# The first attention of a two-layer decoder: new weights for mixing the next group's maxima with the present group's units

## Chip, cores and metric

The kernel runs on one core of one Trainium2 chip. The metric is the time of one execution on the device in microseconds (us); a smaller number is better. Engines are called as in the profile: PE is TensorE, PEld its weight load, DVE is VectorE, ACT is ScalarE, POOL is GpSimd, and SP is SyncE, which here issues the transfers.

## The reference

The input x has 4 batches of 1024 tokens with 256 channels, and six blocks are applied in turn, each as `x = x + f(layernorm(x))`. Cut to what the change touches, the first of them is:

```python
def L0_attn(x, w_attn, w_proj):            # 16 heads of 16 channels, causal, with alibi
    q, k, v = split(x @ w_attn.T)          # each B x 16 x 1024 x 16
    att = q @ k.T / 4 + slopes * (pos_k - pos_q)
    att = softmax(where(pos_k <= pos_q, att, -inf))
    return (att @ v) @ w_proj.T

x = x + L0_attn(ln(x));  x = x + L0_xattn(ln(x), ctx);  x = x + L0_ffn(ln(x))   # 8-bit activations
x = x + L1_attn(ln(x));  x = x + L1_xattn(ln(x), ctx);  x = x + L1_ffn(ln(x))   # 4-bit blocks
```

The second attention (L1_attn) has squared scores with a decay for each token in place of the exponential; L0_xattn and L1_xattn attend to 77 context rows.

## The kernel before

**The first attention.** `A0(b, after)` handles batch b in four groups of four heads. For a group, `stacks` loads two stacked operands, QS (queries) and KS (keys), from DRAM; each has two buffers. The softmax's row maxima are computed ahead of the main loop: `a0_max` is a generator of 38 steps. A step is one or a few matmuls (L352, and L356 for the mask) into a PSUM tile M of one bank, and a reduction by DVE (L357) into the tile mt. M has two banks, 2 and 3, in turn, shared with the tiles Q of the projections. After 11 steps, and again at the end, `a0_put_max` negates the maxima, transposes them (L381), splits them in two bf16 parts (L383, L384) and sends them by two transfers each into rows 108 and 109 of QS, so that the score matmuls of the main loop subtract them.

`a0_main` is the main loop of a group: 20 units. A unit computes scores of four heads for one block of keys and up to 256 queries into two PSUM tiles S (L401, mask L403; banks 0 and 1 in turn), ACT takes the exponential (L404) into P, and two units later PE multiplies P by the values (L413) into O. `o_out` normalizes.

The weaving is done by generators. While group g runs its 20 units, `nxt(g + 1)` loads the stacks of the next group and yields its 38 maxima steps. In group 2, 12 steps of `after` are mixed in as well, and in group 3 the rest of `after` runs. For batches 0 to 2 `after` is `A0_front(b + 1)`, the projections of the next batch (18 steps) and the maxima of its group 0 (38 steps); for batch 3 it is the front of the second attention. The function that mixes takes the next step from the generator that is least far along relative to its weight:

```python
def weave(a, na, b, nb):
    live = {0: (a, na), 1: (b, nb)}
    ...
        k = min(live, key=lambda k: done[k] / live[k][1])
        try:
            next(live[k][0])
...
            yield from weave(self.a0_main(st, V, y, g, O, pend), 20, side, self.NW[b][g])
```

The main loop's weight is 20, the number of its units; the side's weight is `NW[b][g]`. When one generator ends, the other goes on alone.

**Around it.** `schedule` runs the four `A0` in turn, each woven with the cross attention `XA` (L616 to L637) and feed-forward `F0` (L697 to L754; its down projection is L747, L749, L752) of the batch before, at fixed weights. After that, in the second phase, come the second attention `A1` (scores L898, absolute values by DVE L904 or ACT L902, square L906, decay L909 on POOL, value matmuls L927) woven with `XA` and the last feed-forward `F1`. `A1` uses two banks for its scores as well. Splits in high and low parts are recorded under a helper's lines, L179 and L180, and the three-matmul products under L191.

**Order.** The order in which Python emits instructions isn't the order in which the engines run them: the program is built in `tile.TileContext(nc, schedule_with_timeline_sim=True)`, which places the instructions of each engine's queue itself, within the dependencies, and takes the emission order as a preference. Each engine then runs its queue in order.

Of the kernel before, what the change touches and what calls it, by code (L numbers as in the profile page):

```python
# [90 lines left out]
class Kern:  # L91
    MAGIC = 12582912.0
    LAG0, LAG1 = 2, 2
    GQ, NQ = (2, 2, 2, 2), (12, 12, 12, 12)
    NW = ((25, 25, 38, 38),) * 4

    def const(self, *names):
        for nm, dt in names:
# [371 lines left out]
    def A0(self, b, after):  # L470
# [10 lines left out]
        for g in range(4):  # L481
            box = []
            side = nxt(g + 1, box) if g < 3 else after
            if g == self.GQ[b]:
                side = weave(side, 28, take(after, self.NQ[b]), self.NQ[b])
            yield from weave(self.a0_main(st, V, y, g, O, pend), 20, side, self.NW[b][g])
            if g < 3:
# [670 lines left out]
def take(g, n):  # L1158
    for _ in range(n):
        if next(g, g) is g:  # L1160
            return
        yield


def weave(a, na, b, nb):

    live = {0: (a, na), 1: (b, nb)}
    done = [0, 0]
    while live:
# [3 lines that stand above are left out]
            done[k] += 1  # L1173
        except StopIteration:
            del live[k]
        yield
# [149 lines left out]
```

## Time and profile before

| | us |
|---|---|
| median of 3 runs | 2410.97 (2407.53 to 2416.93) |
| the profiled execution's own time | 2408.58 |
| its span, first to last instruction | 2406.8 |
| PE busy | 2141.5 (89%) |
| DVE busy | 1692.2 (70%) |
| ACT busy | 1639.2 (68%) |
| POOL busy | 1198.2 (50%) |

In the trace the four main loops of batch 0 lie between 105 and 335 us, batches 1 to 3 each take a little over 300 us until 1274 us, the second attention runs until 2260 us, and the feed-forward of the last batch ends the span. A row of waits names the engine and tile that waited, the engine and tile that ended the wait, the sum in us, the number of waits and the longest one. A row of a timeline has start, duration and engine, and in brackets the idle time ahead of it with what ended it.

### The profile page before, as it was taken

What the parts mean: (1) busy time and instruction counts of PE and PEld (TensorE: products, weight loads), DVE (VectorE), ACT (ScalarE), POOL (GpSimd) and SP (SyncE); (2) the same over time, 40 slices, a digit from 0 to 9 for tenths busy, and PEclk for the clock granted to TensorE, in tenths of its full rate; (3) what the DMA queues carried; (4) which work ended last, traced back from release to release, by engine and by line L of the source; (5) the groups of instructions that cost most, each with busy time, mean ns of one, the idle gap of its engine ahead of it and who ended that gap; (6) DMA issues with size and microseconds to landing.
All of it is one profiled execution on the core that took longest, in us unless ns stands there. A gap on an engine that the chain in (4) does not pass through costs nothing.

```text
span 2406.8 us, 51445 instructions
## 1 busy us (share of the span) xinstructions
PE 2141.5 (89%) x19110; PEld 1510.9 (63%) x19110; DVE 1692.2 (70%) x3781; ACT 1639.2 (68%) x4173; POOL 1198.2 (50%) x1942
## 2 busy tenths in 40 slices
PE   6798899998999998899988988889988998899876
PEld 4454457755666654576656766567766766676675
DVE  4666657677766786776775677777867787777766
ACT  4365446676766676565778878987678777888542
POOL 7121313154331352412545458766867788775664
PEclk9899999999999999899989999999989999999988
DMA  8667331223841236231262224512241223542000
GB/s 260 199 193 211 116 90 44 66 61 108 242 135 44 64 111 188 69 73 41 81 185 53 71 71 129 149 38 56 98 111 43 56 74 119 105 98 71 10 10 18
DMA packets 182697, 238.45 MB, mean 99 GB/s; under 512 B 16198, under 2 KB 165846, under 8 KB 175958
## 3 DMA queue, kind: packets, MB, share of 16 engines
q1 hardware_dynamic: 182446, 235.15, 34.8%
q8 instruction: 151, 2.47, 0.4%
q14 instruction: 100, 0.82, 0.1%
HBM read 152.62 MB, written 82.21 MB: 98 GB/s over the span
## 4 chain that ended last, share of the span: by engine, by line
PE 59%; DVE 14%; DMA 8%; POOL 7%; ACT 7%; issue 3%; SPq 1%; POOLq 0%; DVEq 0%; ACTq 0%
PE T L191 10%; PE W L191 8%; PE O L413 7%; PE O L927 5%; PE S L401 5%; PE Q L191 4%; PE M L352 4%; PE S L898 3%; DVE P L904 2%; DVE s_mt L357 2%; PE W L630 1%; PE T L723 1%; DMA wst<-in_L_xattn_Wq 1%; POOL P L909 1%; ACT P L906 1%
## 5 line engine op out<-in xcount | busy, mean ns | idle before, releaser
L357 DVE TENSOR_REDUCE s_mt<-M 128x1 f32<-128x512 f32 (+3 forms) x608 | 386.2, 655 | 137.9 <-PE M L356 100.0
L404 ACT ACTIVATE P<-S 128x512 f32<-128x512 f32 (+1 forms) x640 | 342.4, 563 | 154.7 <-PE S L401 78.5
L906 ACT ACTIVATE P<-P,eps 128x1024 f32<-128x1024 f32 x320 | 344.5, 1082 | 57.2 <-DVE P L904 52.6
L904 DVE TENSOR_REDUCE P<-S 128x512 f32<-128x512 f32 (+1 forms) x480 | 284.8, 610 | 75.4 <-PE S L898 60.7
L352 PE MATMUL M<-KS,QS 108*128 108x512 bf16 (+3 forms) x768 | 225.8, 341 | 48.2 <-DVE s_mt L357 23.9
L191 PE MATMUL T<-R,xX 128*128 128x352 f32 (+1 forms) x1136 | 246.7, 331 | 4.8 <-ACT E L619 1.4
L898 PE MATMUL S<-QS,KS 96*128 96x256 bf16 (+1 forms) x1280 | 217.9, 269 | 36.9 <-DVE P L904 34.5
L401 PE MATMUL S<-QS,KS 110*128 110x256 bf16 (+1 forms) x1280 | 230.4, 267 | 16.9 <-ACT P L404 13.7
L413 PE MATMUL O<-P,V 128*32 128x256 f32 (+1 forms) x2560 | 240.1, 377 | 0.8 <-ACT P L404 0.6
L622 POOL TENSOR_TENSOR E<-E,s_xsm 128x616 f32<-128x616 f32 x64 | 77.9, 1217 | 323.7 <-DVE s_xsm L620 261.3
L191 PEld LDWEIGHTS T<-R,xX 128*128 128x128 f32 x1136 | 183.0, 190 | 24.7 <-ACT E L619 5.4
L191 PE MATMUL W<-R,xph 128*128 128x256 f32 (+1 forms) x952 | 185.4, 292 | 6.5 <-DVE xpl L180 4.8
L909 POOL TENSOR_TENSOR P<-P,y 128x512 f32<-128x512 f32 x128 | 165.1, 1299 | 34.0 <-ACT y L871 17.4
L619 ACT ACTIVATE E<-T,s_xmx 128x77 f32<-128x77 f32 x512 | 159.6, 334 | 28.6 <-DVE s_xmx L616 26.5
L401 PEld LDWEIGHTS <-KS 110*128 110x128 bf16 x1280 | 107.2, 100 | 105.6 <-issue 60.3
L927 PE MATMUL O<-P,VsJ 128*32 128x128 f32 x3584 | 168.2, 282 | 5.3 <-ACT P L906 4.8
L898 PEld LDWEIGHTS <-KS 96*128 96x128 bf16 x1280 | 101.8, 99 | 110.2 <-issue 88.9
L191 PEld LDWEIGHTS W<-R,xph 128*128 128x128 f32 (+1 forms) x952 | 149.5, 192 | 17.8 <-DVE xpl L180 6.9
L352 PEld LDWEIGHTS <-QS 108*128 108x128 bf16 x768 | 68.3, 100 | 128.0 <-issue 100.4
L191 PE MATMUL W<-R,xpl 128*128 128x256 f32 (+2 forms) x476 | 139.6, 293 | 1.0 <-DVE xpl L180 1.0
L730 POOL TENSOR_TENSOR R<-wst 128x256 f32<-128x256 f32 x128 | 92.3, 732 | 88.0 <-DVE wst L729 82.8
L179 ACT ACTIVATE xph<-W 128x512 fp32r<-128x512 f32 (+2 forms) x180 | 79.3, 458 | 80.1 <-PE W L633 32.8
(351 smaller groups left out, 5660.0 us busy)
## 6 DMA issues: line engine op xcount, KB each, us to landing
QS<-dr SPq DMA_DIRECT2D x144, 192.0 KB
KS<-dr SPq DMA_DIRECT2D x72, 384.0 KB
dr<-qp SPq DMA_DIRECT2D x32, 768.0 KB
MD<-R SPq DMA_DIRECT2D x24, 616.0 KB
UD<-R SPq DMA_DIRECT2D x24, 512.0 KB
R<-MD SPq DMA_DIRECT2D x32, 308.0 KB
X<-in_x SPq DMA_DIRECT2D x16, 512.0 KB
dr<-qp SPq DMA_DIRECT2D x32, 256.0 KB
```

The source lines that it names most:

```text
L191: nc.tensor.matmul(out, x, y, start=first and n == 0, stop=last and n == len(seq) - 1)
L352: nc.tensor.matmul(Sv[:, x, 0:w], QS[:108, i // 4, hh, i % 4 * 128 : i % 4 * 128 + 128], KS[:108, hh, k0:k1], start=x == 0, stop=not diag ...
L357: nc.vector.tensor_reduce(out, Sv[:, :, 0:w], AX.X, ALU.max)
L401: nc.tensor.matmul(S[:, e, 0:w], st[1][:110, hh, j * 128 : (j + 1) * 128], st[0][:110, q0 // 512, hh, q0 % 512 : q0 % 512 + w], start=e == ...
L404: nc.scalar.activation(P[:, 2 * p : 2 * p + 2, 256 - w :], S[:, :, 0:w], AF.Exp)
L413: nc.tensor.matmul(O[0][hh * 32 : hh * 32 + 32, o + o0 : o + 256], V[j // 4][:, j % 4, h * 17 : h * 17 + 32], P[:, hh, o0:], start=c % 2 = ...
L619: nc.scalar.activation(E[:, n * 77 : (n + 1) * 77], Sv[:, k, :], AF.Exp, bias=mx[:, n : n + 1], accum_out=sm[:, n : n + 1])
L898: nc.tensor.matmul(S[:, e, 0:w], st[r][1][:96, hh, j * 128 : (j + 1) * 128], st[r][0][:96, q0 // 512, hh, q0 % 512 : q0 % 512 + w], start= ...
L904: nc.vector.tensor_reduce(Pv, S[:, :, 0:w].unsqueeze(3), AX.X, ALU.max, apply_absolute_value=True)
L906: nc.scalar.activation(Pw, Pw, AF.Square, bias=self.eps1)
L909: nc.gpsimd.tensor_tensor(Pd, Pd, Ds[r, c][:, j - 2 * c], ALU.mult)
L927: nc.tensor.matmul(Oc[rows, o0 : o0 + 128], lhs, P[:, hh, c0 : c0 + 128], start=j == 2 * c and i == 2 * c, stop=fin and i == 2 * c + 1)
```

## The change

One line of constants changes: the weights of the side generators in `A0`, for all four batches. In groups 0 and 1 the weight goes from 25 to 42, in group 2 from 38 to 54 and in group 3 from 38 to 48. The counts of steps are 38 in groups 0 and 1, 38 + 12 in group 2, and 44 in group 3 (8 in batch 3), so that with the new weights every side generator is emitted to its end beside the 20 units of the main loop. What is computed, and with which instructions, stays as it is.

```diff
     GQ, NQ = (2, 2, 2, 2), (12, 12, 12, 12)
-    NW = ((25, 25, 38, 38),) * 4
+    NW = ((42, 42, 54, 48),) * 4
```

## Prediction

> **What bounds the kernel now.** The table of engines by stretch came first, cut where the attention batches change. Columns: length, then busy time of PE, PEld, DVE, ACT, POOL, then the granted clock.
>
> ```profile
> 335.00:642.00 307.00, 288.68 (x2362) 192.58 (x2361) 218.59 (x494) 207.00 (x610) 103.25 (x150) 0.99 0.33 92
> 642.00:949.00 307.00, 294.09 (x2341) 192.38 (x2341) 220.78 (x504) 204.88 (x608) 98.70 (x146) 0.98 0.40 111
> 949.00:1274.00 325.00, 296.04 (x2298) 194.18 (x2298) 230.15 (x525) 206.33 (x615) 119.84 (x182) 0.93 0.34 96
> 1274.00:1500.00 226.00, 202.85 (x2089) 149.47 (x2081) 156.57 (x388) 190.88 (x518) 135.57 (x253) 0.98 0.29 80
> ```
>
> PE is busy 94, 96 and 91% of the time in the first three rows, which are batches 1 to 3 of the first attention. It idles 18 + 13 + 29 = 60 us in 939. DVE and ACT are near 70%. After 1274 us, in the second attention, PE idles more (23 of 226 us). So I asked next what ends PE's waits.
>
> ```profile
> PE S L898 <- DVE P L904: 34.5, 58, 4.3
> PE M L352 <- DVE s_mt L357: 23.9, 49, 2.0
> PE S L401 <- ACT P L404: 13.7, 16, 3.6
> PE M L352 <- DMA KS<-c_alk: 5.4, 2, 4.4
> PE S L401 <- DMA QS<-VsJ: 2.4, 5, 0.8
> ```
>
> Columns: sum, times, longest. The second row is what the change is about: a maxima step waits until DVE has reduced the bank it is to overwrite. It costs 23.9 us in the whole kernel, in 49 of 608 steps. The first row, in the second attention, is larger. Last the timeline, at a place where maxima steps really stand alone (start, duration, engine):
>
> ```profile
> 293.58 8.20 DVE L357 TENSOR_REDUCE s_mt<-M 128x1 f32<-128x512 f32 x13
> 294.31 0.38 PE L352 MATMUL M<-KS,QS 108*128 108x512 bf16 x1 [0.22 <-DVE s_mt L357]
> 294.91 0.38 PE L352 MATMUL M<-KS,QS 108*128 108x512 bf16 x1 [0.22 <-DVE s_mt L357]
> 295.51 0.38 PE L352 MATMUL M<-KS,QS 108*128 108x512 bf16 x1 [0.22 <-DVE s_mt L357]
> ```
>
> Alone, a step comes every 0.60 us, PE works 0.38 and waits 0.22, while DVE runs its reductions (0.63 us each) without a gap.
>
> **Part one, the emission order.** A maxima generator yields 38 steps against 20 units of the main loop. At the old weights (25) about 25 of them are emitted beside the units; numbering the tiles in order of creation gives 14, 14, 12 and 7 maxima steps behind the last unit of groups 0 to 3, 181 over the 15 group boundaries. With 42, 42, 54, 48 the count is 0 everywhere. If all 181 stood alone, they would cost PE 181 x 0.22 = 40 us. The wait row says 23.9, and that is all that can be won at this place.
>
> **Part two, what the queues make of it.** The framework puts the instructions in its own order. I laid the built queues of the two kernels side by side. Behind the last score matmul of each group, PE's queue of before holds 9, 12, 21, 16 / 20, 7, 34, 16 / 19, 9, 21, 18 / 21, 5, 17 maxima steps, 245 in all. In the changed kernel it holds 9, 12, 21, 16 / 20, 3, 30, 17 / 20, 5, 19, 19 / 18, 4, 17, which is 230. So 181 moved steps become 15 in the queue. In batch 0 the main loop and the maxima stand exactly as before; the burst of the timeline is still there, twelve steps in a row. Those leftover steps mostly aren't alone: PE meets the next group's scores between them, which is why only 49 of 608 wait. Instructions, shapes and counts are the same on every engine, DMAs too: none added, none removed, so busy time is priced at nothing gained or lost. SP's queue shifts by 8 places at most. The transfer that carries a group's maxima back (QS) keeps its cover: between the last maximum and the first score that needs it, PE's queue loses 1.1 us at worst and gains up to 7, so the row of 2.4 us stays.
>
> **Part three, the price of the shuffle.** The reordering runs on to the end of the program, also where no source line moved. I priced the matmuls of each line by its busy time, overlaps counted once, over its columns (scores 0.255 us, maxima 0.288 us, scores of the second attention 0.289 us per 512 columns). Then I summed, along PE's queue, by how much the work between two uses of one thing falls short of the time that thing needs, choosing the need so that the sum of before meets its wait row.
>
> Maxima banks, need 0.9 us (a reduction of 0.65 and its signals): 24.1 before (row: 23.9), 25.9 after: +1.8.
>
> Score banks of the second attention, need 0.9 (reduction of 0.61): 32.7 before (rows: 34.5, and 1.4 behind ACT), 44.5 after: +11.8. Gaps under 0.3 us go from 25 to 41 of 640.
>
> Score banks of the first attention, need 0.9: 8.8 to 9.3, +0.5 (row: 13.7).
>
> The down projection of the first feed-forward, whose matmuls need the 1.02 us copy of L749, need 1.8: 5.6 before (row: 6.2), 11.1 after: +5.5.
>
> P before the value matmuls L927, need 2.5: 11.5 before (rows: 5.1 and 4.8), 15.5 after: +4.
>
> The KS transfer that opens a group's maxima, and can only start when the scores two groups back have let the buffer go. The two waits of the row KS <- c_alk are 1.0 and 4.4 us, at places where PE's queue holds 12.0 and 7.4 us of work between, so the need is about 12.4. In the changed queue the distances of batches 1, 2 and 3 are 9.7, 8.5 and 8.8 us (before 12.0, 13.5 and 7.4): 2.7 + 3.9 + 3.6 = 10.2 against 5.4: +4.8.
>
> The others that I summed go both ways by 1 to 2 us.
>
> The full sum is +28.4 us. It is an upper end, because a stall on PE lets DVE and ACT run ahead and so shortens the next one, and the P and down-projection entries lie in chains that other entries touch. The lower end is 0, all absorbed, or below it: -24 if the maxima waits went after all. I take +13, a little under half: PE is the fullest engine in the first three rows (94, 96, 91%), where a stall stays, but has 10% idle in the second attention, where the largest entry lies.
>
> The profiled execution took 2408.58 us (span 2406.8 and 1.8 around it), 2.4 below the median of 2410.97. 2408.58 + 13 = 2421.6 in a profiled run; against the median, **2424**, slower by 0.54%.
>
> One rule speaks for more room than the wait row: the Trainium skill, "Perfetto Trace Analysis", Identifying the Most-Contended Engine, says that matmul busy time tells little about headroom and that the share of weight loading tells it better. That share is 192.6 of 307 us here, 63%, and by the rule all of the 40 us of part one could come back and the time be 2371. The trace backs half of it: in the burst PE's 0.38 us matmul is followed by an idle 0.22, so at that place there is room, but the same page's advice to look for the gaps leads to the row of 23.9 us, and I keep the row.
>
> **Rivals.** *Within 0.5%: absorbed.* The framework undoes the change, and the shuffle costs next to nothing, 2411 to 2420. For it: 15 of 181 steps moved in the queue; half of DVE's instructions stand within 4 places of where they were in all but one of 16 stretches; ACT is at 84% between 1274 and 1500 us, and where ACT sets the pace a PE stall costs nothing. Against it: every large entry of the sum has the same sign. It is so if L898 grows by 12 and other waits in the second attention shrink by as much.
>
> *Faster by over 0.5%.* The change does what it says on the chip: the maxima steps that still wait find other work, the row of 23.9 falls to 8 or less, and the later shuffle is neutral: 2411 - 16 = 2395; with the row at nothing, 2387. It decides from 12 us of that row on. For it: from 300 us on, 18.7 us of the row remain, and the spacing in batch 1 loosens (7.5 to 6.0). Against it: batches 2 and 3 tighten (2.3 to 4.1, 4.1 to 5.7), and batch 0 can't gain.
>
> *Slower by the full sum.* Nothing is absorbed, as PE can't pass a matmul that waits: 2411 + 28 = 2439. Two banks serve all scores of the second attention, so each late reduction holds all that is queued on PE behind the next score: value matmuls, feed-forward, projections.
>
> **How the numbers follow.** About 0.5%, 12 us, is what a measurement of this kernel can tell from no change (three runs lay 9.4 us apart). The forecast, +12 to +20: 0.30. The full sum and about it, over +20: 0.17. Absorbed, within 12 us either way: 0.40. Faster rival: 0.13. So slower 0.47, same 0.40, faster 0.13. Since cases of both signs hold much, the likeliest one's own range is 2423 to 2431. The 8-in-10 range reaches from a part of the faster rival, 2400, to the full sum, 2439.
>
> **What would show it.** Right: maxima wait 20 to 28 us; L898 <- P L904 at 40 to 48 us; idle before L752 at 8 to 12; KS <- c_alk at 8 to 12, in three waits; PE's busy time within 10 us of 2141.5; the burst of twelve steps in batch 0 still there. Wrong: a maxima wait under 10 us would mean that spacing in the queue doesn't decide it; a row L898 at or below 34 us with a slower kernel would put the loss elsewhere; PE's busy time moving by more than 15 us would mean that order changes the price of a matmul, which I left out; a KS row above 20 or a QS row above 10 us would mean that a moved transfer, not a bank, decides.

## The result, and the profile after

The changed kernel takes 2439.68 us (median of 4 runs, 2438.59 to 2443.28) against 2412.89 (2407.53 to 2416.93) for the kernel before in the same comparison: a ratio of 1.0118, 95% interval 1.0091 to 1.0146. It is slower by 27 us, twice the forecast's loss and 0.7 us above the end of the range. The profiled execution took 2439.42 us, with a span of 2437.6.

The page's row of engine times of the changed kernel (busy us, share of the span, instructions):

```profile
PE 2157.5 (89%) x19072; PEld 1521.0 (62%) x19110; DVE 1701.5 (70%) x3781; ACT 1640.9 (67%) x4173; POOL 1200.6 (49%) x1942
```

PE is busy 16 us longer than before with the same matmuls (the profile records 38 fewer of them). The table of engines by stretch of the changed kernel, at the cuts of the prediction (length, busy PE, PEld, DVE, ACT, POOL, granted clock):

```profile
335.00:642.00 307.00, 288.70 (x2342) 194.32 (x2350) 217.88 (x493) 207.05 (x610) 102.44 (x148) 0.98 0.33 91
642.00:949.00 307.00, 289.41 (x2234) 190.44 (x2242) 210.06 (x478) 195.03 (x588) 95.66 (x142) 0.97 0.35 97
949.00:1274.00 325.00, 291.61 (x2266) 187.93 (x2278) 233.24 (x537) 208.46 (x614) 118.41 (x173) 0.93 0.38 105
1274.00:1500.00 226.00, 204.08 (x2083) 149.50 (x2081) 149.03 (x369) 185.10 (x504) 127.67 (x248) 0.98 0.26 69
```

In the second row the stretch that held 2341 matmuls before now holds 2234, and PE idles 18 us instead of 13: batch 2 falls behind here. PE's waits in the changed kernel (sum, times, longest):

```profile
PE S L898 <- DVE P L904: 39.1, 65, 4.7
PE M L352 <- DVE s_mt L357: 28.1, 55, 5.6
PE S L401 <- ACT P L404: 18.0, 21, 4.2
PE M L352 <- DMA KS<-c_alk: 6.9, 2, 3.8
PE S L401 <- DMA QS<-VsJ: 4.1, 5, 2.6
```

All five rows rose, by 1.5 to 4.6 us, the row that the change is about among them. The timeline of the changed kernel still has the burst at the end of batch 0, as forecast:

```profile
296.92 8.20 DVE L357 TENSOR_REDUCE s_mt<-M 128x1 f32<-128x512 f32 x13
297.66 0.38 PE L352 MATMUL M<-KS,QS 108*128 108x512 bf16 x1 [0.22 <-DVE s_mt L357]
298.26 0.38 PE L352 MATMUL M<-KS,QS 108*128 108x512 bf16 x1 [0.22 <-DVE s_mt L357]
```

**Where the 27 us are.** The record of the granted clock has only two values, 1.0 and 0.5 (a value between them in a table is a mean over a window). If PE works half as fast at 0.5, a span splits into PE's idle time; half of the time in which PE was busy at 0.5, which is what the half clock cost; and the rest, which is the matmul work at full clock. Two more profiles of each kernel (runs 13 to 16 below) give means of three:

| us | span | work at full clock | cost of the half clock | PE idle |
|---|---|---|---|---|
| before, first profile | 2406.8 | 2062.9 | 78.6 | 265.3 |
| before, mean of three | 2409.4 | 2060.9 | 84.9 | 263.6 |
| changed, first profile | 2437.6 | 2060.8 | 96.8 | 280.1 |
| changed, mean of three | 2434.8 | 2061.6 | 94.4 | 278.8 |

The difference of the means is 25.4 us: 15.2 of idle, 9.5 of half clock, 0.7 of work. By place, again as means of three profiles: start and batch 0 +1, batch 1 +1.5, batch 2 +11.5, batch 3 +4.5, and everything from the second attention on, where no source line changed, +7.

The split is an account and no more. Matmuls that follow one another do run about half as fast at 0.5 (two score matmuls L401 of 256 columns start 0.112 us apart at 1.0 and 0.213 at 0.5, medians of the six profiles), but one of them by itself goes from 0.272 to 0.421 us, by a factor of 1.55. And in each kernel the work at full clock reads lower the more half clock a profile holds: before 2063, 2061, 2058 at a cost of 79, 85, 92, changed 2064, 2061, 2060 at 87, 97, 100. So the half clock seems to cost some of these microseconds less than the table says.

One of the new stalls, in batch 2, shows how such a loss is made. Timeline of the changed kernel, first SP's transfers, then the compute engines:

```profile
646.44 1.90 SPq L323 DMA_DIRECT2D QS<-dr  x4
648.38 0.90 SPq L320 DMA_DIRECT2D KS<-dr  x2
...
656.79 0.65 SPq L534 DMA_DIRECT2D wst<-in_L_xattn_Wq  x1
```

```profile
665.02 0.62 POOL L537 TENSOR_SCALAR wst<-wst 128x512 f32<-128x512 f32 x1 [8.35 <-DMA wst<-in_L_xattn_Wq]
665.67 0.63 ACT L538 ACTIVATE xph<-wst 128x512 fp32r<-128x512 f32 x1 [5.24 <-POOL wst L537]
666.73 1.06 ACT L404 ACTIVATE P<-S 128x512 f32<-128x512 f32 x2
667.35 0.37 PE L401 MATMUL S<-QS,KS 110*128 110x128 bf16 x2 [4.21 <-ACT P L404]
```

SP issues a weight load of the cross attention, the first part of it at 656.79 us, behind the group's stacks and, between the rows shown, two pairs of stores (MD at 650.23, UD at 654.10); POOL, which needs it, starts at 665.02. ACT's next instruction is the copy of that weight (L538). ACT idles 5.24 us ahead of it, with the exponential queued behind it, and PE waits 4.21 us for the score bank that the exponential is to free. PE's wait is booked under the exponential; at the end of the chain stands a transfer. Its place behind the stacks isn't enough for a stall, though: in the kernel before, the same load stands behind the same stacks and stores, too, issued at 656.27 us, but POOL starts at 661.68 and ACT's copy after an idle time of 1.72 us. The clock follows. Windows of 3.4 us of the changed kernel around the stall (after the length: busy PE, PEld, DVE, ACT, POOL; the granted clock is the third number from the end):

```profile
660.10:663.50 3.40, 3.05 (x26) 1.74 (x23) 1.40 (x3) 0.33 (x1) 0.00 (x0) 1.00 1.00 343
663.50:666.90 3.40, 0.00 (x0) 0.00 (x0) 0.38 (x1) 1.23 (x3) 1.14 (x2) 0.99 0.54 170
666.90:670.30 3.40, 2.95 (x15) 1.86 (x18) 0.72 (x2) 2.74 (x7) 1.98 (x2) 0.50 0.03 7
670.30:673.70 3.40, 3.40 (x23) 1.57 (x16) 2.42 (x5) 0.74 (x3) 0.00 (x0) 0.50 0.00 0
673.70:677.10 3.40, 3.36 (x25) 2.85 (x25) 2.76 (x7) 2.48 (x6) 0.00 (x0) 1.00 0.50 204
```

Here the half clock lasts 6.8 us, in which PE is busy for 6.35: that costs 3.2 us by the split, beside the 4.2 of the stall, and no row of waits names it. Five more stalls of 2 us and over in batches 1 to 3 are new or longer in all three profiles of the changed kernel: at 491 us (2.1, queries of QS), 681 (2.6, QS), 820 (3.1, KS), 982 (5.6, a maxima reduction on DVE behind L1005, which waits for a weight of the last feed-forward; 2.0 before) and 995 (2.3, the transposed maxima). One of before's, 2.1 us at 1231, is gone. With the 4.2 that is some 16 us of stalls more in the first attention. PE's idle time in batches 1 to 3 rose by 12 us in the means of three (62.0 to 73.9), so smaller waits shrank by some 4. Whether these stalls are the cause is what run 18 below asks.

### The profile page after: what moved, and what is told of

Same layout as the page of the kernel before. It is cut to its first block, busy times and chain, and to the rows that moved or that the text cites. A ratio compares the mean times of both kernels' runs of the same rounds, so it can differ in the third digit from the quotient of the medians.

```text
span 2437.6 us, 51393 instructions
## 1 busy us (share of the span) xinstructions
PE 2157.5 (89%) x19072; PEld 1521.0 (62%) x19110; DVE 1701.5 (70%) x3781; ACT 1640.9 (67%) x4173; POOL 1200.6 (49%) x1942
## 4 chain that ended last, share of the span: by engine, by line
PE 59%; DVE 14%; DMA 8%; ACT 7%; POOL 7%; issue 3%; SPq 1%; POOLq 0%; ACTq 0%; DVEq 0%
PE T L191 10%; PE W L191 8%; PE O L413 7%; PE Q L191 5%; PE O L927 5%; PE S L401 4%; PE M L352 4%; PE S L898 3%; DVE P L904 2%; DVE s_mt L357 2%; DMA wst<-in_L_xattn_Wq 2%; PE W L630 1%; PE T L723 1%; ACT P L906 1%; PE M L356 1%
## 5 line engine op out<-in xcount | busy, mean ns | idle before, releaser
L404 ACT ACTIVATE P<-S 128x512 f32<-128x512 f32 (+1 forms) x640 | 340.9, 561 | 157.4 <-PE S L401 89.5
L904 DVE TENSOR_REDUCE P<-S 128x512 f32<-128x512 f32 (+1 forms) x480 | 285.5, 611 | 79.8 <-PE S L898 60.1
L352 PE MATMUL M<-KS,QS 108*128 108x512 bf16 (+3 forms) x768 | 229.0, 344 | 55.7 <-DVE s_mt L357 28.1
L898 PE MATMUL S<-QS,KS 96*128 96x256 bf16 (+1 forms) x1280 | 218.9, 270 | 45.3 <-DVE P L904 39.1
L401 PE MATMUL S<-QS,KS 110*128 110x256 bf16 (+1 forms) x1280 | 230.4, 268 | 23.7 <-ACT P L404 18.0
L619 ACT ACTIVATE E<-T,s_xmx 128x77 f32<-128x77 f32 x512 | 159.4, 334 | 28.1 <-DVE s_xmx L616 26.6
L898 PEld LDWEIGHTS <-KS 96*128 96x128 bf16 x1280 | 104.1, 100 | 117.5 <-issue 96.6
L401 PEld LDWEIGHTS <-KS 110*128 110x128 bf16 x1280 | 106.2, 100 | 109.7 <-issue 62.0
L927 PE MATMUL O<-P,VsJ 128*32 128x128 f32 x3584 | 166.5, 284 | 5.0 <-ACT P L906 3.9
L730 POOL TENSOR_TENSOR R<-wst 128x256 f32<-128x256 f32 x128 | 94.4, 747 | 95.6 <-DVE wst L729 66.7
```

The costliest lines, as they stand in the source:

```text
L352: nc.tensor.matmul(Sv[:, x, 0:w], QS[:108, i // 4, hh, i % 4 * 128 : i % 4 * 128 + 128], KS[:108, hh, k0:k1], start=x == 0, stop=not diag ...
L401: nc.tensor.matmul(S[:, e, 0:w], st[1][:110, hh, j * 128 : (j + 1) * 128], st[0][:110, q0 // 512, hh, q0 % 512 : q0 % 512 + w], start=e == ...
L404: nc.scalar.activation(P[:, 2 * p : 2 * p + 2, 256 - w :], S[:, :, 0:w], AF.Exp)
L619: nc.scalar.activation(E[:, n * 77 : (n + 1) * 77], Sv[:, k, :], AF.Exp, bias=mx[:, n : n + 1], accum_out=sm[:, n : n + 1])
L898: nc.tensor.matmul(S[:, e, 0:w], st[r][1][:96, hh, j * 128 : (j + 1) * 128], st[r][0][:96, q0 // 512, hh, q0 % 512 : q0 % 512 + w], start= ...
L904: nc.vector.tensor_reduce(Pv, S[:, :, 0:w].unsqueeze(3), AX.X, ALU.max, apply_absolute_value=True)
```

## The experiments

Four theories stood against each other. *Emission*: what counts is how many steps are emitted beside the units, for better or worse. *Queues*: the sum of part three of the prediction, made again for every variant from its built queue, tells the loss. *Lottery*: any change of the weights deals a new order to all engines, and the loss has little to do with what was moved. *Transfers*: the loss is that of transfers that SP issues late. *Handed-down*, in runs 17 and 18, is the lottery with a place: a changed order of one batch is handed on to the stages behind it, so that the loss needn't lie where the weights changed.

**1 to 4: parts of the change, less of it, and its opposite.** These four were timed together, against a median of 2406.46 of the kernel before. Run 1 takes the new weights for groups 0 to 2 only:

```diff
-    NW = ((25, 25, 38, 38),) * 4
+    NW = ((42, 42, 54, 38),) * 4
```

> The change in groups 0 to 2 alone (weights 42, 42, 54, 38): 160 of the 181 maxima steps that were emitted alone are now beside a unit. Queue theory (the time follows how closely PE's queue packs dependent work; the same sum over the queue as in the prediction is 92.9 us here, 88.1 before, 116.5 for the whole change): +5 us, 2418. Emission theory (the loss comes of the maxima being emitted beside the units, in proportion to the steps moved): 160/181 of the loss, +24, 2437. Lottery theory (any other order of these queues is slower by some amount that neither sum tells): anything from +5 to +30.

Run 2 goes about half way:

```diff
-    NW = ((25, 25, 38, 38),) * 4
+    NW = ((33, 33, 46, 43),) * 4
```

> Weights half way (33, 33, 46, 43): 96 of the 181 steps moved. Queue theory: sum 104.4 against 88.1, so +16 us, 2429. Emission theory: 96/181 of 27, +14, 2427. This run can't part these two, but it parts both from a lottery. The maxima wait should be 25 to 29 us by the queue theory (its own sum goes from 24.1 to 26.8).

Run 3 goes the other way in groups 2 and 3:

```diff
-    NW = ((25, 25, 38, 38),) * 4
+    NW = ((25, 25, 25, 25),) * 4
```

> The opposite step: weights 25 in all four groups, so that 256 steps instead of 181 are emitted alone. Emission theory: a gain of 75/181 of 27 us, -11, 2402. Queue theory: sum 101.9 against 88.1, +14, 2427.

Run 4 leaves batch 0 as it was:

```diff
-    NW = ((25, 25, 38, 38),) * 4
+    NW = ((25, 25, 38, 38),) + ((42, 42, 54, 48),) * 3
```

> The change in batches 1 to 3 alone; batch 0 keeps 25, 25, 38, 38. In batch 0 the whole change had left PE's queue as it was but for the preparation of weights. Emission theory: 134 of 181 steps moved, +20, 2433. Queue theory: sum 97.8, +10, 2423; the score banks of the second attention (35.0 against 44.5 for the whole change) should show a wait row of 34 to 38 us instead of 39.

Measured: run 1 2443.67 us, ratio 1.0144 [1.0112, 1.0175], +37; run 2 2422.91, 1.0071 [1.0048, 1.0094], +16.5; run 3 2412.34, 1.0019 [1.0005, 1.0034], +6; run 4 2426.63, 1.0073 [1.0045, 1.0102], +20. Less of the change loses more (run 1), and the opposite doesn't gain. The queue sum meets run 2 and misses the rest, run 1 by 32 us. The emission theory meets run 2 (+14) and run 4 (+20) and misses run 1 (+24) and run 3 (-11). PE's waits of run 1 show why no sum over waits could have told its loss:

```profile
PE S L898 <- DVE P L904: 28.4, 52, 3.6
PE M L352 <- DVE s_mt L357: 23.6, 49, 3.9
PE S L401 <- ACT P L404: 16.5, 22, 3.7
```

The two largest rows are *smaller* than in the kernel before (34.5 and 23.9), and PE idles 261.7 us, 2 less than before's mean, yet the span is 24 us longer: by the split, 12.8 of it is half clock (97.7 against 84.9), and 13 is work, which here doesn't stay constant. This is a single profile, and the half clock's term differs by 13 us between profiles of one queue (runs 13 to 16). What is sure is that PE's busy time rose by 26 us (2171.7 against 2145.7); why it rose in this order is open.

**5 and 6: a change that means nothing.** The weight of groups 0 and 1 goes down or up by one. That moves 8 steps of emission:

```diff
-    NW = ((25, 25, 38, 38),) * 4
+    NW = ((24, 24, 38, 38),) * 4       # run 5;  26 in run 6
```

> Weights 24, 24, 38, 38: eight more steps are emitted alone than before (189 for 181). Emission theory: a gain of 8/181 of 27 us, about -1. Queue sum: 94.4 against 88.1, so +6. Lottery theory (another order is slower by an amount that has nothing to do with how many steps stand alone, much of it in the second attention): +5 to +20. Built with 27 in place of 24, which moves 16 steps the other way, POOL's and SP's queues come out the same as with 24 and the sum is the same 94.4, so this run stands for both signs of the change.

> Weights 26, 26, 38, 38: eight steps fewer alone (173). ACT's queue is that of before up to its place 2700 of 3396, deep in the second attention; so the first attention should take the same time within 3 us. Emission theory: +1. Queue sum: 86.4 against 88.1, so -2. Lottery theory: the whole difference, of up to 10 us either way, lies behind 1600 us, in a stage whose source this doesn't touch.

Measured against 2413.25: run 5 2433.54, ratio 1.0083 [1.0054, 1.0111], +20; run 6 2427.78, 1.0066 [1.0042, 1.009], +14.5. A nudge of one loses over half of what the whole change loses, in both directions. This is what the lottery says, though for run 6 it had named up to 10 us; neither the emission theory (1 us) nor the queue sums (+6, -2) come near. Run 6 even loses it far from the edit. Engines by stretch, kernel before:

```profile
0.00:1804.00 1804.00, 1624.05 (x13878) 1095.70 (x13879) 1249.19 (x2800) 1216.47 (x3209) 778.45 (x1263) 0.96 0.39 112
1804.00:2406.80 602.80, 517.41 (x5235) 415.17 (x5233) 442.99 (x982) 422.72 (x967) 419.71 (x679) 0.95 0.24 61
```

and run 6:

```profile
0.00:1806.00 1806.00, 1626.95 (x13842) 1102.65 (x13880) 1248.69 (x2800) 1215.45 (x3209) 778.32 (x1263) 0.96 0.40 112
1806.00:2422.70 616.70, 536.72 (x5233) 426.72 (x5231) 443.69 (x982) 424.01 (x966) 417.86 (x679) 0.93 0.23 59
```

The stretches meet at the start of the third of the four batches of the second attention, and up to there run 6 is within 2 us of before. Nearly all of the loss comes in the last 600 us: PE's busy time +19, its idle time *less* (80.0 against 85.4), the granted clock 0.93 against 0.95. So the loss isn't one of PE's waits. Nor can it be put down to the clock alone: in the two other profiles of the kernel before, the same stretch has a clock of 0.93, too, and takes 608.2 and 606.9 us. Against the mean of the three, 606.0, run 6 loses 11 us there, and why stays open.

**7 and 8: without the framework's reordering.** Old and new weights with the simulated timeline off, so that the queues stay closer to the emission:

```diff
-    with tile.TileContext(nc, schedule_with_timeline_sim=True) as tc:
+    with tile.TileContext(nc, schedule_with_timeline_sim=False) as tc:
```

> The kernel before with the framework's other ordering (schedule_with_timeline_sim off), which follows the emission order more closely: 354 maxima steps stand behind the last scores in PE's queue, against 245. To be read beside the next run. By the queue sum (159.8 against 88.1) it is slower than the kernel before by some 70 us.

> The changed kernel with the same other ordering: 299 maxima steps behind the last scores, 55 fewer than in e7. Emission theory (beside the units is slower): slower than e7 by 20 us or more. The change's own idea (alone is slower, 0.22 us a step): faster than e7 by 55 x 0.22 = 12 us. Queue sum: 159.6 against 159.8, the same within 5 us.

Measured: 2795.32 us with the old weights, 2813.66 with the new (ratios to before 1.158 [1.1551, 1.1608] and 1.166 [1.1631, 1.1687]). Here 55 fewer steps stand behind the last scores (299 against 354), and the row M <- s_mt does fall, from 40.6 to 33.9 us, as the change intends. The kernel is 18 us slower nonetheless: S <- P L404 rises from 10.5 to 18.5 us, and in all PE idles 5 us more and is busy 9 us longer (2386.6 against 2377.3). So what the change intends can be had at its own wait, and is lost again elsewhere. The queue sum, which expected no difference here and run 7 some 70 us above the kernel before, misses both: run 7 is slower by 382. The emission theory, with 20 us or more between the two runs, comes nearest.

**9 and 10: the first attention alone.** The program stops after the first attention; cross attention, feed-forward and second layer are left out.

```diff
-        decoder_kernel(tc, ins, cs, out, phases=phases, nb=nb)
+        decoder_kernel(tc, ins, cs, out, phases=("A0",), nb=nb)
```

> The first attention alone, with the old weights: the other five blocks and their weight preparation are left out, so the output is x after the first block. To be read beside the next run only; some 700 us. Here the framework makes nearly the same queues of the old and the new weights (221 and 224 maxima steps behind the last scores; a nudge to 26 gives a queue equal to the old one, the half-way weights one equal to the new one).

> The same with the new weights. Emission theory: slower than e9 by the share of the loss that lies in the first attention, 15 us or more. Lottery theory (the loss comes of how other blocks' work falls among the maxima): the same as e9 within 0.5%, about 3 us.

Measured: 875.75 us (873.10 to 878.36; expected some 700) with the old weights, 872.46 (867.87 to 876.14) with the new: no loss and no gain that stands clear of the spread. PE's wait for the maxima, old and then new:

```profile
PE M L352 <- DVE s_mt L357: 19.2, 70, 0.8
```

```profile
PE M L352 <- DVE s_mt L357: 16.4, 59, 0.8
```

The row falls by 2.8 us, in one profile each; the same row moved by 2.3 between profiles of the changed kernel. The two queues are nearly the same here (221 and 224 steps behind the last scores), so this pair can't tell whether steps beside the units cost more. It shows that the loss needs the other blocks in the program: without them the new weights hardly change the order, and nothing is lost.

**11 and 12: another queue for the stores.** If SP's order were the cause, taking the stores of prepared weights (UD, MD, wgud and wdd) off SP should help. They are issued from ACT, with old weights (11) and new (12); three places like this one:

```diff
-    nc.sync.dma_start(self.MD[u][:, h2, c], ...)
+    nc.scalar.dma_start(self.MD[u][:, h2, c], ...)
```

> Old weights; the stores of prepared weights (wgud, wdd, MD, UD) are issued from ACT's queue in place of SP's, so that they no longer stand ahead of KS and QS loads. If transfers that queue on SP are what stalls PE in the first attention, its largest stall (8.2 us at 230 us, behind the wgud store) goes, with up to 5 us of half clock after it: -10 us, 2400. If orders are a lottery, that gain is within its spread: anything from 2395 to 2430.

> The same with the new weights. If the loss of the new weights in the first attention comes of transfers on SP's queue, it shrinks here: the second attention starts within 8 us of where it does in e11, where it was 19 us later without this edit. Emission theory: as before, some 15 to 27 us over e11. Lottery theory: either sign, within 20 us of e11.

Measured against 2410.5: run 11 2446.73, ratio 1.0141 [1.0111, 1.0171], +36 where a gain of 10 was expected, although PE's stall at 230 us (8.2, 7.7 and 6.6 us in the three profiles of before) did shrink to 4.2; run 12 2450.99, 1.0165 [1.0134, 1.0197], 4.3 above run 11. The remedy failed. The difference between old and new weights shrinks from 27 to 4, and the second attention starts 5.5 us later in run 12 than in run 11, within the 8 us that the transfers theory had named. But the lottery allowed it as well, and as both orders are new draws, this doesn't show that transfers made the 27.

**13 to 16: the two kernels profiled twice more each**, unchanged, to tell what belongs to the order and what to the execution.

> The kernel before, unchanged, profiled again. If the clock's share belongs to the queue: span within 10 us of 2407, PE idle 260 to 270 us, 190 to 225 us at half clock. If it belongs to the single execution: 205 us at half clock was luck, and a second profile shows 220 to 260.

> As in e13, the same kernel once more. Matmul work at full clock (busy time less half of what lies at half clock) 2061 us within 3 in either case.

> The changed kernel, unchanged, profiled again. If the clock's share belongs to the queue: idle 275 to 285 us, 235 to 265 us at half clock, the five long stalls of the first attention (491, 663, 681, 820 and 982 us) at the same places. If to the execution: half clock anywhere between 205 and 260.

> As in e15, the same changed kernel once more; the matmul work at full clock 2061 us within 3, and the same five long stalls if they belong to the queue.

Measured: times 2411.57, 2413.35; 2432.70, 2437.67. Idle repeats: 265.3, 263.7, 261.9 before and 280.1, 280.3, 276.0 after. The cost of the half clock doesn't: 78.6, 84.6, 91.5 before and 96.8, 86.9, 99.7 after. The same queue varies by 13 us there. So the idle time is a property of the order, and the clock's share of one profile alone can mislead: the first pair gave 18 of 31 us to the clock, the means 9.5 of 25. The work at full clock lies between 2058 and 2064 us. The stalls named above stand in all three profiles of the changed kernel; the one at 663 us is 4.2, 3.2 and 3.6.

**17 and 18: where is it lost?** New weights in batch 2 alone (17), and in batches 0 and 1 alone (18):

```diff
-    NW = ((25, 25, 38, 38),) * 4
+    NW = ((25, 25, 38, 38),) * 2 + ((42, 42, 54, 48),) + ((25, 25, 38, 38),)   # run 17
+    NW = ((42, 42, 54, 48),) * 2 + ((25, 25, 38, 38),) * 2                     # run 18
```

> New weights in batch 2 alone. Emission theory: batch 2 takes 11 us longer than before (305 to 316 us), the whole +7 to +12. Handed-down theory: batch 2 within 2 us of before, since its queue is nearly that of before; what is lost lies behind 1800 us, as in e6 (queue there much the same as e6's): 0 to +16.

> New weights in batches 0 and 1 alone; batch 2 is emitted as before. Emission theory: batch 2 as before, 305 us, the whole +10 to +14 by its 94 steps. Handed-down theory: batch 2 differs from before although its own weights don't, by several us in either sign; 310 to 318 us if the stalls of the changed kernel (weights behind KS and QS loads on SP's queue) come along.

Measured against 2412.29: run 17 2431.42, ratio 1.0075 [1.0053, 1.0096], +19; run 18 2412.53, 1.0010 [0.9989, 1.0031], no loss, though it moves 94 of the 181 steps. Run 17 loses 5 us in batch 2 (309.9 against a mean of 305.2), between the 2 of the handed-down theory and the 11 of the emission theory, where the whole change loses 11.5; and it loses 13 us from the third batch of the second attention on (618.9 against a mean of 606.0), like run 6. In run 18 batch 2 takes 302.7 us, less than before, although 310 to 318 were expected if the stalls came along. ACT's queue in batch 2 differs from before at 2 of 476 places in run 17 and at 322 in run 18, whose batch 2 keeps the old weights: the order changes where it wasn't told to and hardly where it was.

Run 18 also tests the stalls. The one at 663 us is there again (timeline of run 18):

```profile
663.84 0.63 ACT L538 ACTIVATE xph<-wst 128x512 fp32r<-128x512 f32 x1 [5.26 <-POOL wst L537]
664.37 0.61 ACT L538 ACTIVATE xpl<-wst 128x512 fp32r<-128x512 f32 x1
...
665.52 0.37 PE L401 MATMUL S<-QS,KS 110*128 110x128 bf16 x2 [4.23 <-ACT P L404]
```

The same 4.2 us, behind the same copy, and the one at 681 as well. Batch 2 cut at the first exponential of each group, kernel before:

```profile
643.10:713.80 70.70, 67.55 (x548) 45.52 (x547) 49.72 (x108) 45.73 (x131) 24.35 (x35) 1.00 0.55 158
713.80:799.20 85.40, 84.71 (x658) 57.73 (x652) 55.87 (x126) 53.18 (x215) 11.04 (x10) 1.00 0.21 52
799.20:868.40 69.20, 68.43 (x580) 47.07 (x577) 53.58 (x137) 49.48 (x147) 36.68 (x67) 1.00 0.33 89
868.40:949.90 81.50, 73.20 (x573) 42.09 (x570) 61.80 (x136) 55.72 (x115) 26.38 (x35) 0.94 0.52 154
```

run 18:

```profile
645.40:724.10 78.70, 70.89 (x562) 48.66 (x561) 50.27 (x109) 47.34 (x136) 23.24 (x34) 0.96 0.50 140
724.10:804.50 80.40, 79.20 (x667) 58.49 (x665) 57.40 (x132) 52.51 (x217) 11.59 (x10) 1.00 0.24 59
804.50:874.70 70.20, 68.18 (x566) 45.55 (x567) 53.00 (x136) 49.75 (x140) 36.64 (x68) 1.00 0.30 85
874.70:948.00 73.30, 66.11 (x553) 39.02 (x556) 59.41 (x130) 54.72 (x113) 25.86 (x36) 0.98 0.59 178
```

changed kernel:

```profile
647.20:727.00 79.80, 72.24 (x562) 48.61 (x561) 50.29 (x109) 47.46 (x137) 23.18 (x34) 0.94 0.49 138
727.00:812.30 85.30, 84.09 (x677) 60.47 (x675) 59.23 (x136) 52.37 (x217) 12.16 (x10) 1.00 0.21 52
812.30:888.60 76.30, 72.31 (x549) 45.00 (x551) 50.04 (x125) 49.19 (x139) 34.91 (x66) 0.98 0.29 81
888.60:965.50 76.90, 69.44 (x546) 39.99 (x554) 58.97 (x131) 55.31 (x113) 25.57 (x34) 0.96 0.51 151
```

Both orders lose the first group alike, 8.0 and 9.1 us. Run 18 gets 13 back in the second and fourth groups (85.4 to 80.4, 81.5 to 73.3); the changed kernel gets back 4.6 in the fourth and loses 7.1 more in the third, where its stall at 820 us lies. So the first group is longer by a little more than its two stalls (4.2 and 2.6 us), but the stalls at 663 and 681 don't decide the total.

Nor does the half clock as the split has it. Run 18's profile has as much of it as the changed kernel's (a cost of 96 us), 264 us of idle and a span of only 2408.6, because its work at full clock reads 2049 us, 12 less than in either kernel; runs 1 and 12 read 2074 and 2075. Across orders the work isn't constant, so the 9.5 us that the table puts down to the half clock aren't shown to be its doing.

**All orders together.** Steps whose emission was moved, the queue sum, and the measured loss in us:

| run | steps | queue sum | measured |
|---|---|---|---|
| the change | 181 | +28 | +27 |
| 1 | 160 | +5 | +37 |
| 4 | 134 | +10 | +20 |
| 2 | 96 | +16 | +16.5 |
| 18 | 94 | +7 | 0 |
| 17 | 47 | 0 | +19 |
| 6 | 8 | -2 | +14.5 |
| 5 | -8 | +6 | +20 |
| 3 | -75 | +14 | +6 |

Neither column orders the last one. The steps go a little better with it than the queue sum (rank correlation 0.6 against 0.05 over the nine rows), but runs 5, 6 and 18 stand against a price per step, and nine rows are few. Of these nine orders other than that of the kernel before, eight are slower, by 6 to 37 us, and one is equal; none is faster, so no version that beats both is at hand.

## Why the prediction was right or wrong

**Right: the direction, and that the change undoes itself in the queues.** The maxima wait stayed (28.1 us, just above "20 to 28"; 27.3 in the mean of three), the burst in batch 0 stayed, and no gain came. The rival "faster" fell. Of the other signs, the idle time before L752 came in (9.9 us behind L749), L898 <- P L904 fell just short (39.1), and KS <- c_alk (6.9, in two waits) and PE's busy time didn't.

The time of 2371 that the prediction estimated from the Trainium skill's rule on weight loading ("Perfetto Trace Analysis", Identifying the Most-Contended Engine) lies 69 us below the measured one: the share of weight loading stayed (63 and 62% of the span), and none of the orders tried won any of the 40 us.

**Wrong: the size, at the step "busy time is priced at nothing gained or lost".** As a figure for idle time the +13 was good: PE's idle rose by 15.2. What was missing is PE's busy time, which rose by 16.0 us in the profile and by 10.3 in the mean of three, with the same instructions. My own mark for "order changes the price of a matmul, which I left out" was 15 us: the first profile passes it, the mean doesn't. By the split 9.5 of the 10.3 are half clock; that the clock makes them isn't shown (run 18), and which property of the order does stays open. The term was in reach: the view by stretches already showed a granted clock of 0.93 in batch 3, which the sum left out.

**Right for the wrong reason: the full sum.** It came to +28.4, the loss is 27, and that is chance. Item by item, in means of three profiles each:

| wait, us | forecast | measured |
|---|---|---|
| L898 <- P L904 | +11.8 | +5.6 |
| before L752 (copy of L749) | +5.5 | +2.7 |
| before L927 (P) | +4 | -2.8 |
| KS <- c_alk | +4.8 | +2.4 |
| maxima banks | +1.8 | +3.4 |
| S <- P L404 | +0.5 | +4.5 |
| QS <- VsJ, before maxima and scores | 0 | +4.8 |

The first five rows, which make up nearly all of the sum, rose by 11.3 together where it had 27.9, so "a little under half" was a good figure for them as a whole, though not row by row. The last two were put at 0.5 and at nothing ("so the row of 2.4 us stays") and rose by 9.3.

The spacing sum saw only how close two uses of a buffer stand in PE's queue. It can't see ACT or DVE held at the head of their queue by an instruction of another block, which is what the long waits S <- P L404 at 663 us and for the maxima at 982 us are. I had priced SP at nothing because it shifts "by 8 places at most". A weight load that comes behind a group's stacks in SP's queue held ACT for 5.2 us and PE for 4.2, where the same load had held ACT for 1.7 before. Runs 1 to 6, 17 and 18 show no power of the sum over these orders.

**What decides, as far as it is shown.** The edit is a new draw of the whole program's order, and the order before was a favourable one among the ten that were timed: a nudge of one in a weight loses 14.5 or 20 us, and half of the change that moves 94 steps loses nothing. That a new order costs this much by itself is shown; that nothing of the 27 us belongs to the moved steps as such is not. Single orders differ by up to 9 us either way within one group of one batch, partly as stalls and partly as half clock. Not shown: which property makes an order good, why the stretch from the third batch of the second attention to the end takes 603 to 608 us in the profiles of before and of the changed kernel but 617 to 623 in runs 1, 5, 6 and 17, and how much of the half clock would go if the stalls went. To take away one stall and keep the order of all the rest was not tried.

## What to carry to other kernels

Where a framework orders the queues, an edit of the emission order is a new draw for the whole program, so time a null edit (a weight moved by one) before you believe in the mechanism of any other; here the null edit moved the time by 0.7 to 0.8%, more than any term of the sum. Split a span into work at full clock, cost of the half clock and idle time before you look for waits, take several profiles for the middle term, and don't take the split for a cause: the work term isn't the same in every order. When PE waits for an engine that had time, look at what stands at the head of that engine's queue: it may be another block's copy, waiting for a transfer.

## What the runs showed of the hardware

The half clock doesn't need an idle PE. The granted clock changes only on a grid of 3.413 us. In the three profiles of before and the three of the changed kernel there are 29 to 37 stretches of half clock, in all 205 to 256 us of a run, and each begins after a window of the grid in which PE was busy at most about 0.7 of the time, mostly under 0.65; only two to six windows under 0.55 in each profile weren't followed by one. The busy share alone doesn't decide, as 15 to 23 windows under 0.65 in each profile weren't either. The clearest case is the burst of maxima steps itself. Windows on the grid, changed kernel:

```profile
294.82:298.23 3.41, 2.99 (x26) 1.12 (x25) 2.44 (x5) 1.55 (x4) 2.62 (x4) 1.00 0.22 77
298.23:301.64 3.41, 2.26 (x6) 0.57 (x6) 3.41 (x6) 0.00 (x0) 0.89 (x1) 1.00 0.50 173
301.64:305.05 3.41, 2.81 (x5) 0.79 (x5) 3.25 (x6) 0.00 (x0) 0.00 (x0) 0.50 0.25 80
```

In the second window PE does a step of 0.38 us every 0.60 and never idles for longer than 0.22 us; it is busy 2.26 of 3.41 us, 66%, and the clock halves in the next window. The same burst does so in all six profiles of the two kernels, at 61 to 66% busy. The windows before the clock came back were busy for 0.78 or more of the time; not every such window brought it back (one of 0.99 didn't).

The Trainium skill ("TensorE: Matmul & The Clock Gate", Part 1) gives the clock two states and puts the lower one after an idle window of about 3.4 us. The two values and the length of the window agree with these profiles; "idle" doesn't, as 66% busy, in gaps of 0.22 us, was little enough. What the half clock costs also depends on the place: in the burst, where DVE sets the pace, a longer matmul partly fills time that PE would have idled, and a step comes every 0.69 us at half clock (301.84 to 303.21 us, two steps) against 0.60.
